# Order of outputs, scores, denominators and products in the first and ninth burst of a batch

## The chip, the cores and the metric

The kernel runs on one core of a Trainium2 chip, as one launch. The metric is the device time in microseconds (us). The kernel before takes 2444.21 us in the median of 3 runs.

TensorE (PE in the profile, its weight loads PEld) multiplies matrices into PSUM. VectorE (DVE) and ScalarE (ACT) do the elementwise work, GpSimd (POOL) a little of it, and SyncE (SP) issues most transfers. Each engine works through its own list of instructions in order and waits for others by semaphores.

## The reference

The inputs are 16 batches of 1024 nodes with 256 channels and one 1024 x 1024 adjacency. Layer 0 is a graph product that makes queries, and an attention of 4 heads with them; layer 1 is a graph network of two linear layers with batch norms. Each adds its input and ends in a layer norm. The change lies in layer 0:

```python
c_adj = jnp.mean(fea, axis=1)                       # fea: x transposed, [B, C, N]
diff = c_adj[:, None, :] - c_adj[:, :, None]
A = jnp.abs(jnp.abs(jax.nn.sigmoid(diff) - 0.5) - 0.5) * 2.0
A_s = (A + jnp.transpose(A, (0, 2, 1))) * 0.5
Wg = adj[None, :, :] * A_s
g = jax.nn.relu(jnp.einsum('bcn,bnm->bcm', fea, Wg) * para.reshape(1, C, N))
q = jnp.transpose(g, (0, 2, 1)).reshape(B, N, h, hd).transpose(0, 2, 1, 3)
kv = (x @ kv_w).reshape(B, N, 2, h, hd).transpose(2, 0, 3, 1, 4)
k, v = (kv[0], kv[1])
attn = jax.nn.softmax(jnp.einsum('bhnd,bhmd->bhnm', q, k) * scale, axis=-1)
out = jnp.einsum('bhnm,bhmd->bhnd', attn, v)
x = _layernorm(x + out.transpose(0, 2, 1, 3).reshape(B, N, C), axis=-1)
```

## The kernel before, in words

Attention of a batch is cut into 32 units: two pairs of heads, two halves of the queries (512 each), eight blocks of 128 keys. The eight units of one pair and one half are a group. A unit has two steps on TensorE. `scores` (L1045 to L1059) makes the scores of 128 keys against 512 queries for two heads, as matmuls of 64 by 64 that share the array four at a time (`ps`, L1053), and ScalarE takes their exponentials into a tile `p` (L1058). `outputs` (L1061) multiplies the values by `p` into two PSUM tiles `po`, summed over the group's eight units (L1074), and VectorE adds `p` to the group's sum of exponentials `acc` (L1082 and L1084). At a group's end ScalarE copies one `po` to `oT`, VectorE adds the other (L1091, L1092) and `squares` transposes and stores the result (L1103, L1104).

The softmax's denominators are made once for a pair of heads, in `normalise` (L1115): TensorE sums the two groups' `acc` over the partitions, by four products with a column of ones of 128 rows and 32 columns (`den`, L1122; eight instructions, four for each `acc`), ScalarE copies the PSUM tile to `drow` (L1128), and SyncE stores it and loads it back as columns `dcol` (L1130, L1135). `residual` (L1140) takes their reciprocals later.

Work is ordered by hand. The scheduler is off for TensorE, ScalarE, VectorE and SyncE (L1312), so the order in the program is the order in each engine's list. Two units make a burst, 16 bursts a batch. The loop at L1383 goes over the bursts j, with b the batch and u the burst's place in it (0 to 15). Each turn emits the scores of burst j, then by `back(j - 1)` the outputs of the burst in front (L1346), and then a piece of the next batch's preparation, which depends on u:

- u = 0: `values` and `keys` of the batch that begins its queries next (`pv` L995, `pk` L982), interleaved with steps of the graph weights (`weights_abs` L827 and `weights_tanh` L832 on ScalarE, `weights_adj` L836 on VectorE). After the first values and the first keys the list `sums` is run, and then a load of outputs (L1412 to L1414).
- u = 4: products 1, 2 and 3 of the graph product, made of seven half-size products (`product`, L873, `pga` to `pgd`, L885; 3.4 us of TensorE each), and the last keys.
- u = 5 to 7: `between` (L922), subtractions on VectorE that prepare the weights for the remaining products (L871), and at u = 7 also the left operand `S` (L858).
- u = 8: product 6, then `next_first`, which is the column means of a later batch on VectorE and their transfers on SyncE (L799 to L806), then `sums`, then products 7, 5 and 4 (L1430 to L1441).

The list `sums` holds one call of `normalise`. `back` puts it there when it has emitted the last outputs of a pair of heads, which is in the turns u = 0 (second pair of the batch in front) and u = 8 (first pair). The last batch has its own branch (L1397): there `sums` runs right behind `back` and before anything else.

PSUM has two buffers for scores (`tile_s`), two for outputs (`tile_o`) and two that products, values, keys and denominators share (`tile_t`). There are four `p` tiles (L738) and two `acc` tiles.

Of the kernel before, what the change touches and what calls it, by code (L numbers as in the profile page):

```python
# [515 lines left out]
def fast_path(  # L516
# [20 lines left out]
    B, N, C = x.shape  # L537
# [197 lines left out]
    with (  # L735
# [36 lines left out]
        def load_rest():  # L772
            for n in range(2, NCH, 2):
                nc.sync.dma_start(adj_s[:, n : n + 2, :], adj_src[:, n : n + 2, :])
                if n == 2:
                    load_x(1)
            nc.sync.dma_start(para_s, para.rearrange("o (c p) i j -> p (o c) (i j)", p=P))
# [395 lines left out]
        def run(fs, k):  # L1173
            for f, a in fs[:k]:
                f(*a)
            del fs[:k]
# [135 lines left out]
        with tc.manual_schedule(  # L1312
            engines={
                mybir.EngineType.PE, mybir.EngineType.Activation, mybir.EngineType.DVE,
                mybir.EngineType.SP,
            }
        ):


            first, steps, side = prologue(0)  # L1320
            run(first, 5)
            load_rest()
            next_first, next_steps, next_side = prologue(1)
            for i in range(8):
                run(steps, 1)
                if i > 3:
                    run(side, 2)
                if i == 6:
                    run(next_first, 1)
                    load_squares(1, 0)  # L1330
            run(side, 99)
            for n in range(NCH):
                run(steps, 1)
                if n in (1, 5):
                    run(next_first, 1)
                if n == 1:
                    load_squares(1, 1)
                if n:
                    run(next_side, 3)
            for _ in range(8):  # L1340
                run(next_steps, 1)
                run(next_side, 1)
            full, sums, late = [], [], []
            rows_of = []

            def back(j):  # L1346

                for i in bursts[j]:
                    outputs(i)
                b, pr, qh, m = units[bursts[j][-1]]  # L1350
                if m == NCH - 1 and qh == 1:
                    sums.append((normalise, (b, pr)))
                    for q in range(2):
                        full.append((residual, (b, pr, q)))
                    if pr == PAIRS - 1:
                        for f in (statistics_x1, finish_x1):
                            for ns in (range(NCH // 2), range(NCH // 2, NCH)):
                                late.append((f, (b, ns)))

            last, before_last = {}, {}  # L1360
            for u, todo in (
                (6, (load_x1l, 0)), (7, (load_weights,)), (9, (degrees,)), (10, (row_of_degrees,)),
                (11, (transpose_weights, 0)), (12, (transpose_weights, 1)),
                (13, (add_identity,)), (14, (scale_adjacency, 0)),
            ):
                last.setdefault(u, []).append((todo[0], todo[1:]))
            for f, places in (
                (transpose_adjacency, (9, 11, 13, 15, 17, 19, 21, 23)),
                (load_adjacency_squares, (6, 9, 9, 11, 13, 15, 17, 19)),
                (adjacency_columns, (11, 13, 14, 16, 18, 20, 22, 24)),  # L1370
            ):
                for m, u in enumerate(places):
                    where = before_last if u < PERB else last
                    where.setdefault(u % PERB, []).append((f, (m,)))
            for u, n in ((9, 6), (10, 7)):
                before_last.setdefault(u, []).append((adjacency_rows, (n,)))
            for i in range(4):
                ns = range(2 * i, 2 * i + 2)
                last.setdefault(8 + i, []).append((statistics_x1, (B - 2, ns)))
            for u, ns in ((13, range(2)), (14, range(2, 5)), (15, range(5, NCH))):  # L1380
                last.setdefault(u, []).append((finish_x1, (B - 2, ns)))
            last[15].append((load_x1l, (1,)))
            for j in range(len(bursts)):  # L1383
                b, u = j // PERB, j % PERB
                for i in bursts[j]:
                    scores(i)
                if u == 0:
                    steps, side = next_steps, next_side
                    next_first, next_steps, next_side = [], [], []
                if j:  # L1390
                    back(j - 1)
                if u in (5, 9, 13):
                    run(rows_of, 1)
                if u == 5 and b + 2 < B:
                    load_x(b + 2)
                    next_first, next_steps, next_side = prologue(b + 2)
                if b == B - 1:  # L1397
                    if u == 0:
                        run(sums, 1)
                        run(rows_of, 1)  # L1400
                    elif u in (2, 13):
                        run(full, 2)
                    elif u == 8:
                        run(sums, 1)
                    elif u == 3:
                        late.clear()
                elif u == 0:
                    for i in range(7):
                        if b:
                            run(steps, 1)  # L1410
                            run(side, (2, 3, 2, 3, 2, 2, 99)[i])
                        if i == 1:  # L1412
                            run(sums, 1)
                            run(rows_of, 1)  # L1414
                elif u < 4:
                    if u == 1:
                        run(full, 2)
                    else:
                        run(late, 1)
                    run(side, 99)  # L1420
                elif u == 4:
                    p = st[b + 1]["graph"]["p"]
                    keys_last = steps[:1] if b else []
                    del steps[: len(keys_last)]
                    p[1]()
                    run(keys_last, 1)
                    run(late, 2)
                    p[2]()
                    p[3]()
                elif u == 8:  # L1430
                    p = st[b + 1]["graph"]["p"]
                    p[6]()
                    run(next_first, 1)
                    run(sums, 1)
                    if b == B - 2:
                        adjacency_diagonal()
                        for n in range(6):
                            adjacency_rows(n)
                    p[7]()
                    p[5]()  # L1440
                    p[4]()  # L1441
                elif u < 8:
                    st[b + 1]["graph"]["between"](u)
                else:
                    if u == 9 and b + 2 < B:
                        load_squares(b + 2, 0)
                    if u == 11:
                        run(full, 2)
                    if u == 12:
                        run(next_first, 1)  # L1450
                        if b + 2 < B:
                            load_squares(b + 2, 1)
                    if u == 15:
                        run(next_first, 1)
                    run(next_side, 1)
                if b == B - 2:
                    run(before_last.get(u, []), 9)
                if b == B - 1:
                    run(last.get(u, []), 9)
            j = len(bursts)  # L1460
            back(j - 1)
            for m in range(NCH):
                if m == 0:
                    for k in range(3, NCH):
                        scale_adjacency(k)
                elif m < 4:
                    adjacency_sums(m - 1)
                elif m == 4:
                    adjacency_sums(3)
                aggregate_first(m)  # L1470
                if m == 1:
                    run(sums, 1)
                if m == 4:
                    run(full, 2)
            late.clear()
            x_last = st.pop(B - 1)["x"]
            last_statistics, last_apply = layernorm_steps(x_last, f"l0_{B - 1}")
            last_statistics()
# [583 lines left out]
```

## Time and profile before

| | |
|---|---|
| median of 3 runs | 2444.21 us (2444.15 to 2444.86) |
| the profiled execution's own time | 2444.04 us |
| its span, first to last instruction | 2442.3 us |
| TensorE busy | 2401.4 us, 98% |
| VectorE busy | 1860.5 us, 76% |
| ScalarE busy | 1239.0 us, 51% |
| granted TensorE clock | 0.997 of full speed |

Times in the profile are in us from the first instruction. A line of the timeline has the start, the length, the engine, the line of the kernel, the operation, the tile written and those read, their shapes, how many instructions are merged in it, and in brackets the idle time of the engine in front of it with what ended that idle time. A line of the chain of waits has start, length, engine, tile and line. [...]the length in a timeline line runs some 0.2 us into the next one; the distance from start to start is what a stretch costs.

### The profile page before, as it was taken

What the parts mean: (1) busy time and instruction counts of PE and PEld (TensorE: products, weight loads), DVE (VectorE), ACT (ScalarE), POOL (GpSimd) and SP (SyncE); (2) the same over time, 40 slices, a digit from 0 to 9 for tenths busy, and PEclk for the clock granted to TensorE, in tenths of its full rate; (3) what the DMA queues carried; (4) which work ended last, traced back from release to release, by engine and by line L of the source; (5) the groups of instructions that cost most, each with busy time, mean ns of one, the idle gap of its engine ahead of it and who ended that gap; (6) DMA issues with size and microseconds to landing.
All of it is one profiled execution on the core that took longest, in us unless ns stands there. A gap on an engine that the chain in (4) does not pass through costs nothing.

```text
span 2442.3 us, 32486 instructions
## 1 busy us (share of the span) xinstructions
PE 2401.4 (98%) x12294; PEld 1015.7 (42%) x12294; DVE 1860.5 (76%) x2561; ACT 1239.0 (51%) x1539; POOL 462.8 (19%) x467
## 2 busy tenths in 40 slices
PE   9999999999999999999999999999999999999996
PEld 5343443443434434434344343344444444444444
DVE  5688878878888788788888888955566556479978
ACT  7376675765765756657657667420110111144568
POOL 0021112111211211112112112422122122010026
PEclk9999999999999999999999999999999999999999
DMA  5124232332242332332322326321221221265558
GB/s 164 40 40 87 56 50 70 69 52 65 41 81 57 49 79 61 53 70 53 66 62 40 87 46 92 90 103 69 86 103 69 88 102 69 86 222 177 180 202 357
DMA packets 437877, 221.96 MB, mean 91 GB/s; under 512 B 361552, under 2 KB 411216, under 8 KB 431568
## 3 DMA queue, kind: packets, MB, share of 16 engines
q1 hardware_dynamic: 418400, 169.20, 28.2%
q0 software_dynamic: 2528, 33.57, 3.3%
q10 hardware_dynamic: 16784, 17.04, 2.1%
q8 instruction: 98, 1.61, 0.3%
q14 instruction: 67, 0.55, 0.1%
HBM read 136.06 MB, written 83.69 MB: 90 GB/s over the span
## 4 chain that ended last, share of the span: by engine, by line
PE 86%; DVE 9%; ACT 2%; DMA 1%; issue 1%; POOL 0%; POOLq 0%; DVEq 0%; ACTq 0%
PE ps L1053 18%; PE po L1074 18%; PE pgb L885 7%; PE b_agg L1558 4%; PE pga L885 4%; PE c_agg L1558 4%; PE pk L982 4%; PE b_o L1766 3%; PE pv L995 3%; PE a_agg L1558 2%; PE b_h L1590 2%; PE pgc L885 2%; PE pgd L885 2%; PE c_o L1766 2%; PE a_o L1766 2%; PE c_h L1590 2%
## 5 line engine op out<-in xcount | busy, mean ns | idle before, releaser
L1058 ACT ACTIVATE p<-ps 128x1024 f32<-128x1024 f32 x512 | 497.2, 1021 | 183.8 <-PE ps L1053 146.0
L1084 DVE TENSOR_TENSOR acc<-acc,p 128x1024 f32<-128x1024 f32 x384 | 499.9, 1302 | 53.4 <-ACT p L1058 28.5
L1053 PE MATMUL ps<-qT,kT 64*64 64x512 f32 x4096 | 488.1, 592 | 0.3 <-ACT p L1058 0.3
L1074 PE MATMUL po<-p,v 64*64 64x512 f32 x4096 | 485.3, 589 | 0.0
L1149 POOL TENSOR_TENSOR o<-o,r_all 128x512 f32<-128x512 f32 x62 | 94.8, 1540 | 1162.3 <-DVE r_all L1143 989.0
L1074 PEld LDWEIGHTS po<-p,v 64*64 64x64 f32 x4096 | 158.2, 133 | 281.2 <-issue 274.3
L1053 PEld LDWEIGHTS ps<-qT,kT 64*64 64x64 f32 x4096 | 151.5, 133 | 286.8 <-issue 249.1
L836 DVE SCALAR_TENSOR_TENSOR wg<-wg,adj_s 128x1024 f32<-128x1024 f32 x128 | 149.6, 1216 | 17.6 <-ACT wg L832 17.6
L827 ACT ACTIVATE wg<-crow,ccol 128x1024 f32<-128x1024 f32 x128 | 146.8, 1147 | 0.0
L832 ACT ACTIVATE wg<-wg 128x1024 f32<-128x1024 f32 x128 | 136.0, 1062 | 0.9
L995 PE MATMUL pv<-kvw_s,xT 128*128 128x256 f32 x512 | 125.1, 387 | 0.0
L982 PE MATMUL pk<-xT,kvw_s 128*128 128x512 f32 x256 | 121.9, 598 | 3.1 <-ACT drow L1128 3.1
L995 PEld LDWEIGHTS pv<-kvw_s,xT 128*128 128x128 f32 x512 | 95.7, 191 | 50.3 <-issue 14.2
L895 ACT ACTIVATE qT<-qT 128x512 f32<-128x512 f32 x60 | 37.4, 630 | 156.1 <-DVE qT L898 145.3
L885 PE MATMUL pgb<-wg,S 128*128 128x512 f32 x240 | 111.0, 605 | 0.0
L885 PE MATMUL pga<-wg,x 128*128 128x512 f32 x240 | 109.6, 599 | 0.7 <-ACT qT L908 0.7
L1558 PE MATMUL a_agg<-ahT,x1l 128*128 128x512 f32 x240 | 108.1, 593 | 0.7 <-ACT agg L1300 0.7
L1150 POOL TENSOR_TENSOR x<-x,o 128x512 f32<-128x512 f32 x62 | 107.8, 1749 | 2.4
L1558 PE MATMUL b_agg<-aT,x1S 128*128 128x512 f32 x240 | 107.9, 592 | 0.0
L656 ACT COPY p_agg<-a_agg 128x512 f32<-128x512 f32 x15 | 8.8, 585 | 183.4 <-PE a_agg L1558 183.4
L692 POOL TENSOR_TENSOR x1S<-x1l 128x512 f32<-128x512 f32 x15 | 19.4, 1297 | 353.6 <-PE c_agg L1558 349.6
L1082 DVE TENSOR_TENSOR acc<-p,p 128x1024 f32<-128x1024 f32 x64 | 77.3, 1208 | 7.5 <-ACT p L1058 7.5
(230 smaller groups left out, 3468.5 us busy)
## 6 DMA issues: line engine op xcount, KB each, us to landing
h<-hw POOLq DMA_DIRECT2D x16, 2048.0 KB, 6.7
hl<-h SPq DMA_DIRECT2D x32, 1024.0 KB
x<-x ACTq DMA_DIRECT2D x16, 1024.0 KB
x1l<-x SPq DMA_DIRECT2D x16, 1024.0 KB
xf<-x SPq DMA_DIRECT2D x16, 1024.0 KB
o<-oS SPq DMA_DIRECT2D x62, 256.0 KB
o<-o SPq DMA_DIRECT2D x248, 64.0 KB
x<-in_x_dram SPq DMA_DIRECT2D x15, 1024.0 KB
```

Source lines behind the costliest of these rows:

```text
L827: nc.scalar.activation(w, s["crow"], AF.Abs, bias=s["ccol"][:, n : n + 1])
L832: nc.scalar.activation(w, w, AF.Tanh, scale=0.5)
L836: nc.vector.scalar_tensor_tensor(w, w, 1.0, adj_s[:, n, :], op0=ALU.subtract, op1=ALU.mult)
L885: nc.tensor.matmul(ps, left, right, start=(start and i == 0), stop=(i == NCH // 2 - 1), skip_group_check=True,)
L982: nc.tensor.matmul(ps, kvw_s[:, c, kc * P : (kc + 1) * P], s["xT"][:, c, hs], start=(c == 0), stop=(c == CC - 1),)
L995: nc.tensor.matmul(pt[:, j * C : (j + 1) * C], s["xT"][:, c, n * P : (n + 1) * P], kvw_s[:, c, C : 2 * C], start=(c == 0), stop=(c == CC - 1),
L1053: nc.tensor.matmul(ps[kh * D : (kh + 1) * D, hd * HALF : (hd + 1) * HALF], kT[r, pr, ks], qT[r, pr, qh * HALF : (qh + 1) * HALF], start=Tr ...
L1058: nc.scalar.activation(p, ps, AF.Exp)
L1074: nc.tensor.matmul(g["po"][kh][hd * D : (hd + 1) * D, :], s["v"][r, m, h * D : (h + 1) * D], p[r, hd * HALF : (hd + 1) * HALF], start=(m = ...
L1084: nc.vector.tensor_add(g["acc"], g["acc"], p)
L1558: nc.tensor.matmul(ps, left, right, start=(start and i == 0), stop=(i == NCH // 2 - 1), skip_group_check=True,)
L1766: nc.tensor.matmul(ps, left, right, start=(start and i == 0), stop=(i == 1), skip_group_check=True,)
```

## The change

In the bursts u = 0 and u = 8 of every batch but the last, and but the very first burst of all, `back(j - 1)` is called ahead of the scores of burst j. `sums` is run right behind the scores, ahead of everything else that the turn emits; the two later places where it was run are removed. At u = 0 the load of outputs stays where it was. This concerns 15 turns with u = 8 (batches 0 to 14) and 14 with u = 0 (batches 1 to 14). No instruction is added or taken away.

```diff
             for j in range(len(bursts)):
                 b, u = j // PERB, j % PERB
+                first = j and b < B - 1 and u in (0, 8)
+                if first:
+                    back(j - 1)
                 for i in bursts[j]:
                     scores(i)
                 if u == 0:
                     steps, side = next_steps, next_side
                     next_first, next_steps, next_side = [], [], []
-                if j:
+                if j and not first:
                     back(j - 1)
+                if first:
+                    run(sums, 1)
                 if u in (5, 9, 13):
                     run(rows_of, 1)
...
                         if i == 1:
-                            run(sums, 1)
                             run(rows_of, 1)
...
                     p[6]()
                     run(next_first, 1)
-                    run(sums, 1)
                     if b == B - 2:
                         adjacency_diagonal()
```

In TensorE's list the ninth burst was: scores, outputs of the burst in front, product 6, denominators, products 7, 5 and 4. It becomes: outputs of the burst in front, scores, denominators, products 6, 7, 5 and 4. The first burst was: scores, outputs of the burst in front, values, keys, denominators, values, keys and so on. It becomes: outputs of the burst in front, scores, denominators, then values and keys in turn.

## The prediction

> **What bounds the kernel now.** I read the page's busy times first, then the chain of waits over one batch, then the order of TensorE's and VectorE's instructions in time around a changed place (batch 6), and last the one place in this trace where the denominators already stand directly behind outputs.
>
> ```profile
> PE 2401.4 (98%) x12294; PEld 1015.7 (42%) x12294; DVE 1860.5 (76%) x2561; ACT 1239.0 (51%) x1539; POOL 462.8 (19%) x467
> ```
>
> TensorE is busy in 2401.4 of 2442.3 us. VectorE's 76% is a mean over stages; below, a stretch where it is full decides. The chain of waits at the ninth burst (start, length, what) runs on TensorE alone:
>
> ```profile
> 684.17 1.72 PE ps L1053 x16
> 685.89 1.72 PE po L1074 x16
> 687.60 3.63 PE pgb L885 x8
> 691.23 1.00 PE den L1122 x8
> 692.23 3.63 PE pgb L885 x8
> 695.86 3.43 PE pgc L885 x8
> 699.29 3.43 PE pgb L885 x8
> 702.73 1.88 PE ps L1053 x16
> ```
>
> Scores and outputs cost 1.72 a burst, a product 3.43, and 3.63 where the array has just changed its tile shape: each change into the 128 by 128 shape costs 0.20. Two of them here belong to products, one only because the denominators cut the products in two. In this stretch VectorE has no room (start, length, instruction, idle time in front):
>
> ```profile
> 675.85 2.56 DVE L1084 TENSOR_TENSOR acc<-acc,p 128x1024 f32<-128x1024 f32 x2 [0.58 <-ACT p L1058]
> 678.32 2.49 DVE L871 TENSOR_TENSOR wg<-wg,wg 128x512 f32<-128x512 f32 x4
> 680.73 0.69 DVE L925 TENSOR_TENSOR qT<-qT 128x512 f32<-128x512 f32 x1
> 681.34 2.55 DVE L1084 TENSOR_TENSOR acc<-acc,p 128x1024 f32<-128x1024 f32 x2
> 683.80 2.49 DVE L871 TENSOR_TENSOR wg<-wg 128x512 f32<-128x512 f32 x4
> 686.21 0.68 DVE L858 TENSOR_TENSOR S<-x 128x512 f32<-128x512 f32 x1
> 686.81 2.55 DVE L1084 TENSOR_TENSOR acc<-acc,p 128x1024 f32<-128x1024 f32 x2
> ```
>
> From 675.85, where it last waited (for the exponentials of the sixth burst, so for TensorE), to 689.36 it works without a pause. The last line is the sum over the eighth burst, which the denominators read. Today they start at 691.16 by TensorE's own records: 1.80 after the sum.
>
> At the first burst of a batch TensorE shows one of its few waits:
>
> ```profile
> 637.23 1.06 PE L1122 MATMUL den<-acc,ones 128*32 128x512 f32 x8
> 638.23 1.99 PE L995 MATMUL pv<-kvw_s,xT 128*128 128x256 f32 x8
> 640.45 1.98 PE L982 MATMUL pk<-xT,kvw_s 128*128 128x512 f32 x4 [0.22 <-ACT drow L1128]
> 642.27 1.89 PE L995 MATMUL pv<-kvw_s,xT 128*128 128x256 f32 x8
> ```
>
> Keys wait there for ScalarE's copy of the denominators, which stands behind other ScalarE work and still holds one of two PSUM buffers.
>
> [...]
>
> **The change part by part.** It touches the ninth burst of 15 batches (0 to 14) and the first of 14 (1 to 14), 29 places; batch 15 keeps its order. VectorE's order stays the same everywhere; TensorE, ScalarE and SyncE are reordered.
>
> *Outputs ahead of scores.* The same 32 matmuls of 1.72 + 1.72, exchanged. Outputs of the burst in front now start 1.72 earlier, at 683.99 instead of 685.71, and need that burst's exponentials. The last of those ran 681.66 to 683.60, halves ending at about 682.6 and 683.6; the second unit's outputs begin 0.86 later. Slack 1.30 and 1.25 us, the same at all 29 places: no wait. Scores need the buffers those exponentials read: free. On ScalarE the copy of the outputs now precedes the exponentials, but it is ready 1.95 after the outputs start (685.93) and takes 0.5, before the first scores arrive (685.71 + 1.10 = 686.81): free.
>
> *Denominators ahead of the products, ninth burst.* Gain: one shape change less, 0.20. From 687.53 to the next scores at 702.66 is 15.13 today; without a wait it would be 1.00 + 3.54 + 3.43 + 3.43 + 3.53 = 14.93. Loss: TensorE reaches them at 685.71 + 1.72 + 0.11[...] = 687.54, and the sum is ready at 689.36 as before, since VectorE's queue up to it is unchanged. The first product, 3.63, was the cover, and it now stands behind the wait. What a split of the eight costs is to be seen in batch 15, where they follow outputs and come too early:
>
> ```profile
> 1530.84 2.51 DVE L1084 TENSOR_TENSOR acc<-acc,p 128x1024 f32<-128x1024 f32 x2
> 1532.45 0.14 PEld L1122 LDWEIGHTS den<-acc,ones 128*32 128x32 f32 x4 [0.81 <-issue]
> 1532.45 2.00 PE L1122 MATMUL den<-acc,ones 128*32 128x512 f32 x8
> 1533.40 0.14 PEld L1122 LDWEIGHTS den<-acc,ones 128*32 128x32 f32 x4 [0.81 <-DVE acc L1084]
> 1534.39 1.95 PE L1053 MATMUL ps<-qT,kT 64*64 64x512 f32 x16
> ```
>
> Four, of the older sum, run at once. Four wait for the new sum (ends 1533.35) and start 0.05 later. The next work begins at 1534.39, 1.04 after the sum. So the first product starts at 689.36 + 1.04 = 690.40 instead of 688.54: a stall of 1.86. TensorE is truly idle for only some 0.9 of it. Behind the wait on TensorE stand all four products (13.9 us), then scores; VectorE waits for the first product, with nothing urgent. Later bursts give nothing back, since TensorE waits for no one there. The distance from sum to denominators is 1.80 or 1.81 at twelve of the 15 places, 1.75 in batch 0, and 1.46 in batches 5 and 13. Stalls are thus 12 x 1.855 + 1.92 + 2 x 2.205 = 28.6; less 15 x 0.20 = 3.0, the ninth bursts lose **25.6**.
>
> *Denominators ahead of values and keys, first burst.* TensorE reaches them at 630.05 + 1.72 + 1.83 = 633.60; the sum ends at 633.18. In 13 batches it is at least 0.05 early, in batch 12 late by 0.08 (0.12 lost). From the first values (633.59) to the next scores (647.53) is 13.94 today: 1.83, 1.81, 1.00, 2.22, 1.82, 1.72, 1.72, 1.82. With the denominators in front: 1.00 + 1.83 + 5 x 1.72 + 1.82 = 13.25. That removes a shape change and the wait for the copy, 0.69 in all. The copy now follows the exponentials on ScalarE, at about 634.8 to 635.4, and the keys want its buffer at 636.43: covered by 1 us. What is late next is ScalarE's copy of the second values, which I place at 640.8 to 641.4 against a use at 641.60: 0.1 to 0.2 us of room; with that gone the gain shrinks by what the copy is late. 14 x 0.69 - 0.12 = **9.5** gained.
>
> *The DMA queue.* On SyncE the four stores and four loads of the denominators (1.16 + 2.03 of issuing) move ahead of the column means' four and the row's load at the ninth burst. They end near 696, while the means leave VectorE near 698 then. The row is issued near 700.5 and wanted near 708 (today 697.55 and 706.56). At the first burst their order is unchanged. The store of the outputs stays in front; GpSimd's order is unchanged. Nothing charged.
>
> **Sum.** +25.6 - 9.5 = +16.1 on the profiled execution of 2444.04 (span 2442.3 and 1.7 around it) gives 2460.1. The median of the runs is 0.17 higher; 2460.
>
> **The rivals.** (1) Faster: the denominators don't wait. Then only the gains stay, 14 x 0.69 + 15 x 0.20 = 12.7, hence 2431. It needs the eighth burst's sum to end 1.82 us earlier; that is its point at each ninth burst. For it: first bursts have such room. Against it: 13.5 us of VectorE work in one piece. (2) The gain at the first burst is eaten by the late copy of values or by the sum: at worst 9.5 less, 2470. For it: 0.1 us of room. (3) The resumed half is cheaper, 0.5 instead of 0.98, if the array overlaps it with the first product: 15 x 0.5 = 7.5 less, 2452. Against it: batch 15's 1534.39. (4) Gains and stall cancel: no measurable change, if the stall were 0.85 a place, 2444. Nothing shows it; it needs half of rival 1.
>
> **Chances.** Forecast 0.68, rival 1 0.09, rival 2 0.10, rival 3 0.09, rival 4 0.04. The range takes in rivals 2 and 3, 2452 to 2470, and leaves out 0.13. A measurement tells 0.2%, about 5 us, from no change: faster 0.09, same 0.04, slower 0.87.
>
> **What would show it.** In the new profile: a wait of TensorE's denominators for VectorE's acc of some 0.9 us at 15 places; the eight taking about 2.9 us there instead of 1.07; no wait of pk for drow; the ninth block 1.66 us longer, the first 0.69 shorter. If the denominators of the ninth burst last 1.07, I am wrong on the sign. If pv or pk waits for ScalarE's v or kT, the second term is wrong.

## The result, and the profile after

The changed kernel takes 2479.19 us in the median of 4 runs (2477.87 to 2479.89), the kernel before 2444.18 (2444.02 to 2444.86). The ratio is 1.0143, with a 95% interval of 1.0129 to 1.0156: 35 us slower. The forecast had the direction and one of the causes, and less than half of the size.

The waits of TensorE in the profile after (who waited, for whom, us in total, times, longest) begin with two rows that the kernel before has not:

```profile
PE den L1122 <- DVE acc L1084: 16.3, 15, 1.1
PE pgb L885 <- DVE qT L932: 11.8, 15, 0.8
```

The first was forecast: the denominators wait for VectorE's sum. The second was not: product 7 waits until VectorE has read product 6. Neither row gives the whole cost, because the wait row counts only true idleness; the cost is read from start to start. TensorE's timeline in the ninth burst of batch 6 after the change:

```profile
699.06 1.90 PE L1053 MATMUL ps<-qT,kT 64*64 64x512 f32 x16
700.88 1.05 PE L1122 MATMUL den<-acc,ones 128*32 128x512 f32 x4
703.03 1.05 PE L1122 MATMUL den<-acc,ones 128*32 128x512 f32 x4 [1.09 <-DVE acc L1084]
704.01 3.70 PE L885 MATMUL pgb<-wg,S 128*128 128x512 f32 x8
708.49 3.70 PE L885 MATMUL pgb<-wg,S 128*128 128x512 f32 x8 [0.78 <-DVE qT L932]
712.03 3.60 PE L885 MATMUL pgc<-wg,S 128*128 128x512 f32 x8
715.46 3.60 PE L885 MATMUL pgb<-wg,x 128*128 128x512 f32 x8
718.99 1.52 PE L1053 MATMUL ps<-qT,kT 64*64 64x512 f32 x12
```

From the start of the denominators to the next scores this is 18.11 us, against 15.13 before for the same work. The eight denominators take 3.13 from start to start, in two halves as in batch 15 of the kernel before. Products 6 and 7 take 4.48 + 3.54 = 8.02, where two products on end would be 3.54 + 3.43 = 6.97: 1.05 more.

The chain of waits (start, length, what) ran on TensorE alone here before. Now it comes from VectorE's work of the burst before, enters the denominators by their second half, and leaves TensorE again between the two products (pieces under 0.05 us left out):

```profile
700.51 1.15 DVE acc L1084
701.75 1.23 DVE acc L1084
703.03 1.05 PE den L1122 x4
704.08 3.65 PE pgb L885 x8
707.75 0.70 DVE qT L932
708.49 3.70 PE pgb L885 x8
```

The last three lines are the wait that I missed. VectorE starts to read the tile when product 6 is done, reads for 0.70, and product 7, which adds to the same tile, starts 0.04 later. The load of its first weights stands at the same time in the trace, behind the same wait, so nothing of product 7 ran ahead:

```profile
708.49 0.30 PEld L885 LDWEIGHTS pgb<-wg,S 128*128 128x128 f32 x2 [1.61 <-DVE qT L932]
```

The first bursts did what was forecast. In batch 6 the denominators start at 647.63, the values at 648.63 and the next scores at 660.88: 13.25 from the denominators on, as worked out, against 13.94 before. The wait of keys for the copy of the denominators is gone.

Per batch the sum is: ninth burst 18.11 - 15.13 = +2.98 (14 places) and +2.77 in batch 0, whose denominators take 2.92; first burst -0.69 (14 places). That is 44.5 - 9.7 = +34.8, and the span grew by 2477.7 - 2442.3 = 35.4.

### The profile page after: what moved, and what is told of

Read it like the earlier page. It is cut to its first block, busy times and chain, and to the rows that moved or that the text cites. A ratio compares the mean times of both kernels' runs of the same rounds, so it can differ in the third digit from the quotient of the medians.

```text
span 2477.7 us, 32500 instructions
## 1 busy us (share of the span) xinstructions
PE 2412.1 (97%) x12294; PEld 1022.7 (41%) x12294; DVE 1858.8 (75%) x2561; ACT 1236.3 (50%) x1539; POOL 465.0 (19%) x467
## 4 chain that ended last, share of the span: by engine, by line
PE 80%; DVE 17%; issue 2%; ACT 0%; DMA 0%; POOL 0%; DVEq 0%; POOLq 0%; ACTq 0%
PE ps L1053 14%; PE po L1074 14%; PE pgb L885 7%; PE pv L995 5%; PE b_agg L1561 4%; PE pk L982 4%; PE pga L885 4%; DVE acc L1084 4%; PE c_agg L1561 4%; DVE wg L871 3%; PE b_o L1769 3%; PE a_agg L1561 2%; PE b_h L1593 2%; PE pgd L885 2%; PE pgc L885 2%; PE a_o L1769 2%
## 5 line engine op out<-in xcount | busy, mean ns | idle before, releaser
L1149 POOL TENSOR_TENSOR o<-o,r_all 128x512 f32<-128x512 f32 x62 | 108.1, 1762 | 1182.2 <-DVE r_all L1143 1182.1
L1150 POOL TENSOR_TENSOR x<-x,o 128x512 f32<-128x512 f32 x62 | 95.9, 1565 | 0.2
```

## The experiments

The theory after the result: the loss is two waits of TensorE for VectorE in each ninth burst, one for the sum and one for the reading of product 6; the exchange of outputs and scores costs nothing, and the first burst gains. Rivals: the exchange itself costs; both waits are one and the same backlog of VectorE, so that a cure of one only moves it. Each time stands beside runs of the kernel before on the same chip. Their medians lie between 2444.2 and 2445.0, so a difference between runs that were taken at different times carries up to 0.8 us of that.

**First bursts alone.**

```diff
-                first = j and b < B - 1 and u in (0, 8)
+                first = j and b < B - 1 and u == 0
...
                     run(next_first, 1)
+                    run(sums, 1)
```

> Only the first bursts are changed, the ninth are as before. Theory (two waits of TensorE in the ninth burst: the denominators for VectorE's sum, product 7 for VectorE's reading of product 6): none of them is here, the 0.69 us of 14 first bursts stays gained, 2444.2 - 9.7 = 2434.5. Rival (the exchange of outputs and scores costs time at each place): above 2444.

Measured: 2435.16 us against 2444.49, ratio 0.9963 (0.9949 to 0.9977). The gain of 9.3 is the term of 9.7. Neither of the two new waits is in its profile. This part of the change alone is faster than both kernels, by 0.4% and by 1.8%.

**Ninth bursts alone.**

```diff
-                first = j and b < B - 1 and u in (0, 8)
+                first = j and b < B - 1 and u == 8
...
                         if i == 1:
+                            run(sums, 1)
                             run(rows_of, 1)
```

> Only the ninth bursts are changed. The order of GpSimd's products and sums is that of the kernel before here. Theory: the stall at the denominators is 1.86 as forecast (28.6 in all), product 7 waits 1.05 in each of 15 places (15.8), one shape change less (3.0): 2444.2 + 41.4 = 2485.6. Rival for the extra 0.27 us of stall (it comes from the ninth burst's own new order and not from GpSimd): 2489.

Measured: 2484.51 us, ratio 1.0164 (1.0147 to 1.0181): +40.0 where +41.4 was expected. Its waits of TensorE:

```profile
PE den L1122 <- DVE acc L1084: 12.5, 15, 0.9
PE pgb L885 <- DVE qT L932: 11.8, 15, 0.8
```

The wait for the sum is smaller than in the changed kernel (12.5 against 16.3), and the denominators take 2.86 from start to start and not 3.13. So 0.27 of the stall in the ninth burst comes from the change in the first burst. The ninth is 2.71 longer here than before, 15 x 2.71 = 40.7. Part of the 1.4 that was expected in excess is batches 5 and 13, which stall by 1.86 here like the others and not by 2.205.

**The exchange alone**, with the denominators at their old places.

```diff
-                if first:
-                    run(sums, 1)
```

> Outputs and scores are exchanged at all 29 places, the denominators stay where they were. Theory: no change, 2444.2. Rival (the exchange costs): most of the 35 us, up to 2479.

Measured: 2444.10 us, ratio 0.9998 (0.9990 to 1.0007). The exchange costs nothing that shows within an interval of some 2 us, and the first rival is out.

**The denominators alone**, with the scores still ahead of the outputs.

```diff
-                if first:
-                    back(j - 1)
...
-                if j and not first:
+                if j:
                     back(j - 1)
```

> The denominators are moved as in the changed kernel, but scores stay ahead of outputs at all 29 places. Theory: TensorE reaches the denominators at the same time and waits for the same sum, so all of the loss is here: 2479.2. Rival (outputs and denominators one behind the other without the scores between wait longer, for the sum can't start before the outputs' exponentials): above 2485; rival (the loss needs the exchange): 2444.

Measured: 2479.01 us, ratio 1.0144 (1.0126 to 1.0162). The two rows of waits are those of the changed kernel. All of the loss is in the place of the denominators; whether scores or outputs stand right in front of them makes no difference that shows.

**Product 7 in a tile of its own, first try.** Product 7 goes to a fresh PSUM tile, and nothing carries product 6 over.

```diff
-                product(7, pg["b"], False)
-                nc.vector.tensor_add(q_at(1, H1), pg["b"], q_at(1, H0))
+                pg["e"] = tile_o(f"pge_{b}")
+                product(7, pg["e"], True)
+                nc.vector.tensor_add(q_at(1, H1), pg["e"], q_at(1, H0))
```

> The changed kernel, with product 7 in a PSUM tile of its own, so that it need not wait until VectorE has read product 6; left out of the computation is the sum of products 6 and 7 in one tile (the second query quarter lacks product 6 and another one lacks product 7). Theory: the 1.05 us at 15 places go, 2479.2 - 15.8 = 2463.4. Rival (VectorE as a whole is late, the wait only moves to product 5): 2479.

Measured: 6947.16 us. This tells nothing of the question. The kernel checks the range of its denominators and computes everything again in `general_path` when they leave it, and the page of this run is full of that function's lines, this one at the top:

```profile
L264 PE MATMUL ps<-kT,qT 64*128 64x512 f32 x2048 | 1073.8, 643 | 0.6
```

Leaving a product out had changed the data so far that this other path was run and timed as well.

**Product 7 in a tile of its own, second try.** One addition of VectorE more hands product 6 on, and product 4 follows product 7 into the new tile.

```diff
                 nc.vector.tensor_add(q_at(0, H1), pg["b"], q_at(0, H1))
+                nc.vector.tensor_add(q_at(1, H0), pg["b"], q_at(1, H0))
                 left_last()
...
-                product(7, pg["b"], False)
-                nc.vector.tensor_add(q_at(1, H1), pg["b"], q_at(1, H0))
+                pg["e"] = tile_o(f"pge_{b}")
+                product(7, pg["e"], True)
+                nc.vector.tensor_add(q_at(1, H1), pg["e"], q_at(1, H0))
...
-                product(4, pg["b"], False)
-                nc.vector.tensor_add(q_at(1, H0), pg["b"], q_at(1, H0))
+                product(4, pg["e"], False)
+                nc.vector.tensor_add(q_at(1, H0), pg["e"], q_at(1, H0))
```

> The changed kernel with products 7 and 4 in a PSUM tile of their own, and one more addition on VectorE that carries product 6 into the quarter where it was summed before, so that the output is the reference's again. Product 7 need not wait for VectorE's reading of product 6. Theory: 1.05 us at 15 places go, 2479.2 - 15.8 = 2463.4. Rival (VectorE as a whole is late in the ninth burst, the wait only moves to product 5): 2479.

Measured: 2463.82 us, against 2479.19 for the changed kernel: -15.4 where -15.8 was expected (the spans of the two profiles differ by 15.8). Its timeline of TensorE in the ninth burst of batch 4 still has the wait for the sum and no other:

```profile
500.81 1.05 PE L1124 MATMUL den<-acc,ones 128*32 128x512 f32 x4 [1.10 <-DVE acc L1086]
501.79 3.70 PE L885 MATMUL pgb<-wg,S 128*128 128x512 f32 x8
505.33 3.60 PE L885 MATMUL pge<-wg,S 128*128 128x512 f32 x8
508.76 3.60 PE L885 MATMUL pgc<-wg,S 128*128 128x512 f32 x8
```

The products follow each other by 3.54 and 3.43. VectorE even has more to do, and the wait did not move to product 5: the backlog was not its cause, the shared tile was. From the denominators to the next scores this run takes 17.06, which is 1.05 less than 18.11.

**The sum early.** VectorE's subtractions of the eighth burst move behind its sum.

```diff
                 if first:
                     back(j - 1)
+                    if u == 8:
+                        st[b + 1]["graph"]["between"](7)
...
                 elif u < 8:
-                    st[b + 1]["graph"]["between"](u)
+                    if u < 7:
+                        st[b + 1]["graph"]["between"](u)
```

> The changed kernel, with VectorE's subtractions of the eighth burst moved behind its sum, so that the sum is ready some 3 us earlier and before TensorE reaches the denominators. Theory: the stall at the denominators goes (14 x 2.13 + 1.92 = 31.7) and product 7's wait stays: 2447.5. Rival (both waits come from VectorE's backlog): both go, 2431.7.

Measured: 2447.07 us, ratio to the kernel before 1.0009 (1.0000 to 1.0018). That is -32.1 against the changed kernel, where -31.7 was expected. Its waits of TensorE begin with the other one, unchanged, and have no row of the denominators:

```profile
PE pgb L885 <- DVE qT L932: 11.8, 15, 0.8
```

From the denominators to the next scores it takes 15.98, which is 1.05 more than the 14.93 that was forecast for this stretch without a wait. So the two waits are separate things, and the second rival is out on both sides.

**Both edits together.**

> Both of these edits at once. Theory: neither wait is left, only the gains stay: 2479.2 - 31.7 - 15.8 = 2431.7. Rival (there is a third cost in the new order): above 2440.

Measured: 2432.60 us, ratio to the kernel before 0.9950 (0.9933 to 0.9966). Neither of the two rows is left, and from the denominators to the next scores it takes 14.93, the forecast for no wait. One row is there that neither kernel has, a single wait in the last batch:

```profile
PE po L1076 <- DVE oT L1094: 1.4, 1, 1.4
```

What is left is the gain, forecast at 12.7 where nothing waits, and measured at 11.6 to 12.4 by the two medians of the kernel before. No third cost of the new order shows in the bursts that were changed. This version is faster than both kernels; from the first bursts alone (2435.16) it differs by 2.6 us, about the size of the intervals.

**GpSimd in program order.** The 0.27 that the first burst sends to the ninth asked for a cause. GpSimd is the one engine whose order the scheduler chooses. In the kernel before it normalises one half of the outputs and adds it to x, then the other half:

```profile
651.82 1.99 POOL L1149 TENSOR_TENSOR o<-o,r_all 128x512 f32<-128x512 f32 x1 [30.63 <-DVE r_all L1143]
653.88 2.13 POOL L1150 TENSOR_TENSOR x<-x,o 128x512 f32<-128x512 f32 x1
655.97 1.04 POOL L1149 TENSOR_TENSOR o<-o,r_all 128x512 f32<-128x512 f32 x1
657.09 1.27 POOL L1150 TENSOR_TENSOR x<-x,o 128x512 f32<-128x512 f32 x1
```

After the change it multiplies both and then adds both:

```profile
665.17 3.97 POOL L1149 TENSOR_TENSOR o<-o,r_all 128x512 f32<-128x512 f32 x2 [29.95 <-DVE r_all L1143]
669.10 2.49 POOL L1150 TENSOR_TENSOR x<-x,o 128x512 f32<-128x512 f32 x2
```

VectorE's first statistics of x start 8.52 after the second burst's first scores before, and 9.52 after them now. VectorE carries that microsecond along, loses most of it where it used to wait for the exponentials of the sixth burst (0.58), and ends its sum 0.27 later.

```diff
-                mybir.EngineType.SP,
+                mybir.EngineType.SP, mybir.EngineType.Pool,
```

> The changed kernel, with GpSimd also held to the order of the program in the attention, so that the normalised halves are finished one after the other in the first bursts again, as in the kernel before. Theory: the sums on VectorE come 0.27 us earlier at the ninth bursts' denominators, the stall there is 1.86 and not 2.13, 2479.2 - 14 x 0.27 = 2475.4. Rival (the 0.27 comes from the shorter first burst itself): 2479.

Measured: 2477.79 us, ratio 1.0135 (1.0118 to 1.0151). The cause of the 0.27 is shown: the statistics start at 8.52 again, the denominators take 2.86 at each of the ninth bursts but batch 0's (2.92), and the wait for the sum is 12.5 again instead of 16.3. The time fell by 1.4 only, where 3.8 was expected. The traces tell where the rest is lost: from the denominators of batch 0's ninth burst to those of batch 14's, with 13 of the 14 places between them, this run is 3.5 us shorter than the changed kernel (1382.2 against 1385.7), and from there to the end 2.6 us longer (987.5 against 984.9). The fixed order holds for GpSimd's other work in the attention too; 0.9 of the 2.6 is a new wait of outputs for VectorE's oT in the last batch, the rest is not settled.

## Why the prediction was wrong, point by point

*Outputs ahead of scores cost nothing*: right. The exchange alone measured a ratio of 0.9998.

*The stall at the denominators*: the mechanism and its price were right. The restart 1.04 after the sum, taken from batch 15, holds: with the ninth bursts alone the eight take 2.86, as forecast (1.00 + 1.86), and taking the wait away is worth 32.1 us. In the changed kernel nothing behind the waiting half went ahead of it: in batch 6 the first product and the load of its first weights start at 704.01, 0.98 after that half. The stall there is 2.13 at 14 places and 1.92 in batch 0, 31.7 in all instead of the 28.6 of the forecast. At 12 places that is 0.27 more than forecast, because of the statement "GpSimd's order is unchanged". It is not: GpSimd's order in the first bursts is another one, as shown above. I took it from the fact that no line of its work was edited. At batches 5 and 13 the forecast had 2.205, from later sums in the profile before; those didn't recur in the changed kernel, which has 2.13 there too.

*"Without a wait it would be 1.00 + 3.54 + 3.43 + 3.43 + 3.53 = 14.93"*: this step failed, and it is the larger miss. It prices products 6 and 7 as if they could follow each other. They add into one PSUM tile, VectorE has to read product 6 in between, and the denominators stood there. I had counted them only as a shape change that cuts two products, worth 0.20; they were also the cover of that read, worth 1.05. The sentence "VectorE waits for the first product, with nothing urgent" is the same mistake: the read of product 6 is what VectorE waits to do, and product 7 waits for it. At 15 places this is 15.8 us; a tile of its own gave 15.4 back.

The profile before showed it. VectorE's read of the tile runs from 691.27 to 691.96, within the 1.00 us of the denominators that started at 691.16, and product 7 started at 692.16. The order has the same cover in other places: keys stand between products 1 and 2, which share a tile, and product 5 between 7 and 4. And in one place of the kernel before the cover is missing: in batch 0 no keys stand between products 1 and 2, and product 2 waits there until ScalarE has copied product 1.

```profile
82.04 3.70 PE L885 MATMUL pga<-wg,x 128*128 128x512 f32 x8
86.42 3.70 PE L885 MATMUL pga<-wg,x 128*128 128x512 f32 x8 [0.68 <-ACT qT L908]
```

*The first burst*: right, 0.69 forecast and 0.69 in the records, 9.3 us for the 14 places. The late copy of values that rival 2 feared made no wait, and the 0.12 charged to batch 12 did not appear.

*The clock*: nothing was charged for it, which was an estimate of mine, and the granted clock of the profiled executions was 0.996 after and 0.997 before. The longest wait of TensorE in both is 5.0 us, of its first instruction for the load of x. The longest wait for the sum is 1.1, where some 0.9 was forecast.

With both missed terms the working gives 1.66 + 1.05 + 0.27 = 2.98 for a ninth burst, which is what the trace has. Of the 19 us between 2460 and the measured time, 15.8 are product 7's wait and 3.1 the larger stalls. None of the rivals in the prediction named either term; rival 1's number, 2431, is what the kernel reaches once both waits are gone (2432.60).

## What to carry to other kernels

Before an instruction is moved away from between two others, ask what those two need from each other: work of 1.00 us between two products that add into one PSUM tile hid a read that costs 1.05 when it is bare. A step moved forward also brings its own operands' due time forward; here VectorE was full for 13.5 us in front of it, and a change of VectorE's order moved the sum. Where a scheduler orders one engine, compare its list too, since an edit elsewhere can change it.

## What the runs showed of the hardware

GpSimd's operations on 128 x 512 values took up to twice as long in some places as in others of the same batch: the multiplication 1.99 and then 1.04 us, the addition 2.13 and then 1.27 (kernel before, lines above). VectorE's work beside them differs:

```profile
651.68 3.21 DVE L1084 TENSOR_TENSOR acc<-acc,p 128x1024 f32<-128x1024 f32 x2
656.05 0.43 DVE L620 BATCH_NORM_STATS2 st_l<-x 128x6 f32<-128x256 f32 x1 [1.16 <-POOL x L1150]
```

The first multiplication and the first addition began beside VectorE's sums, the last two ran beside VectorE's statistics. VectorE's sums took longer there as well, 3.21 for two where two take 2.55 elsewhere. Their end is at 654.89, and the first addition ends 1.12 behind it, at 656.01, near the 1.27 of the second. After the change the two additions ran from 669.10 on, behind the end of VectorE's two sums at 668.24 (start 665.03, again 3.21), and took 2.49 for two. So GpSimd and VectorE were slow in the same stretches. No run here was made to find out why, so the cause stays open.

TensorE's times by shape, from start to start in the kernel before: the sixteen 64 by 64 matmuls of a burst's scores took 1.72, the eight 128 by 128 ones of a product 3.43, all with 512 columns. That is 0.11 and 0.43 for one, a quarter, as of four at a time.
